# Seven block products of sums in place of eight for the lookups of an image, with the differences on GpSimd and one ring of eight PSUM banks

## The chip, the cores and the metric

The kernel runs on one core of one Trainium2 chip. The metric is the device time of one execution in microseconds; "before" is the median of three runs.

## The reference

A pre-activation block of two convolutions in which each 3x3 convolution is replaced by a soft lookup. For every channel the 3x3 patch is compared with 16 centroids of 9 values, a softmax over the 16 distances gives weights, and the weights select from a table of 256 outputs.

```python
def amm_conv3x3(x, centroids, w_sub):
    p = patches                                  # [b, n, c, 9]
    d = sum(p*p) - 2*einsum('bncs,cks->bnck', p, centroids) + sum(centroids**2)
    attn = softmax(-d, axis=-1)                  # 16 weights a channel
    lut = einsum('cks,cso->cko', centroids, w_sub)
    return einsum('bnck,cko->bno', attn, lut)

def layer(x):                                    # [16, 256, 28, 28] float32
    out = amm_conv3x3(groupnorm(x), centroids1, wsub1)
    out = relu(bn1(out))
    out = amm_conv3x3(out, centroids2, wsub2)
    out = se(bn2(out))
    return x + relu(out + groupnorm(x))
```

## The kernel before

The sum over centroids is moved in front of the table: a channel's 9 weighted centroid values (a "numerator" each) are divided by the softmax's denominator, and the 256 x 9 quotients of a position are multiplied by `w_sub` (2304 x 256). So an image of a layer is a matrix product of the quotients with `w_sub`, and that product is called the lookup.

**Blocks.** The work of one layer and one image is cut into four blocks: two halves `t` of the 28 rows (14 rows, N = 392 positions) and two halves `hh` of the 256 input channels. A block's quotients are nine tiles q of 128x392 (k = 0 to 8). There are 2 layers x 16 images x 4 = 128 blocks, layer by layer, image by image.

**Order.** All five engines execute one order written out by hand: `at(cluster, place, function, ...)` (L657) files a job under a cluster and a place in it, and the jobs are then issued sorted by both. Each engine takes its own instructions in that order and waits for what it needs. A block j begins in cluster g = 2j, and each cluster does half of a block's logits; an image takes eight clusters. Below, "even" and "odd" clusters are those of the first and the second half of a block. A block passes through:

- `patches` (L283): six DMAs on SP's queue load the shifted rows of 64 channels from a DRAM copy of the padded image (`home1` or `home2`) into one of three patch buffers, three clusters ahead.
- `logits` (L298, cluster g and g+1): 32x32 matmuls into four banks for each quarter `mm` of the block, eight banks a cluster; `exps` (L312) takes the exponential of each bank on ScalarE. In layer 1, for the first quarter of a block with hh = 0, the logits are first copied, turned, reduced to a maximum, reduced by it and turned back on VectorE (`wide_copy`, `wide_turn`, `wide_sub`, `wide_back`, `wide_exp`).
- `num_b`, `split_b`, `join_b`, `recip_dve` (even cluster g+2): the denominators r and the ninth numerator; the join and the reciprocal are on VectorE. Then `spread` (a shuffle of r to the lanes of tile k) and `scale_q` (q times the spread r, both in SBUF), for k = 8.
- `num_a` (L348): the other eight numerators, four banks in cluster g+2 that ScalarE copies (`copy_a`; they are scaled in cluster g+3 by four pairs of `spread` and `scale_q`), and four in cluster g+3 that VectorE multiplies straight from PSUM (`scale_a`).
- `lookup` (L428): for each half t of the rows and each half o of the 256 outputs, nine matmuls of 128x128 by 128x392 for each hh go into one accumulator bank. An image has eight such groups of nine, one a cluster in clusters 5 to 12 counted from the image's first, at place 2.0, after logits and numerators. `evacuate` (L438) reads an accumulator with scale, bias and, in layer 0, ReLU, on ScalarE, at the head of the next cluster.

PSUM has eight banks: one for the accumulator (`p_acc`) and a ring of seven (`p_ring`), which are taken in turn.

**Beside it.** GpSimd normalises the next image (`gn_apply`) and sends stores to DRAM from its own queue: the padded image, the layer-0 results (`to_home2`, an indirect DMA whose row order is a ranking of channels by size). The ranking is made once from image 0: `rank_score`, `rank_row`, `rank_make` and `rank_look` around cluster 13, and the tables of layer 1 are then re-ordered (`prep_codes`, `prep_sub`, `prep_wd0` to `prep_cwb`). In layer 1 `se_hidden`, `se_gate`, `finish` (L640) and `store` end an image: one ScalarE and two VectorE instructions of 128x784 for each half of the outputs.

After the 256 clusters a flag is computed; a loop that does the whole work more slowly (and safely) stands behind it and is not entered with these inputs.

Of the kernel before, what the change touches and what calls it, by code (L numbers as in the profile page):

```python
# [8 lines left out]
F32 = mybir.dt.float32  # L9
# [27 lines left out]
NPT = 3  # L37
# [21 lines left out]
def kernel(  # L59
# [27 lines left out]
    p_acc = ctx.enter_context(tc.tile_pool(name="p_acc", bufs=1, space=PSUM))  # L87
    p_ring = ctx.enter_context(tc.tile_pool(name="p_ring", bufs=7, space=PSUM))
# [23 lines left out]
    d_fl = dram.tile([1, 1], I32, name="d_fl")  # L112
# [5 lines left out]
    epool = ctx.enter_context(tc.tile_pool(name="epool", bufs=24))  # L118
    qpool = ctx.enter_context(tc.tile_pool(name="qpool", bufs=27))
# [4 lines left out]
    def load_x(b, eng=None):  # L124
        t = io.tile([P, NB, HW], F32, tag="xt", name="xt")
        (eng or nc.sync).dma_start(t, x[b].rearrange("(b p) n -> p b n", p=P))
        xs[b] = t
# [22 lines left out]
    def load_ws(l, hh, eng=None):  # L150
        t = wpool.tile([P, NS, C], F32, tag=f"ws{hh}", name=f"ws{hh}")
        eng = eng or nc.sync
        if l == 0:
            eng.dma_start(t, ws1[:, NS * hh : NS * hh + NS, :])
        else:
            eng.dma_start(t[:, 0:8, :], view(d_wa, hh * 8 * P * C, [[C, P], [P * C, 8], [1, C]]))
            eng.dma_start(t[:, 8, :], d_wb[hh * P : hh * P + P, :])
        wts["ws", hh] = t
# [4 lines left out]
    kst = load(konst, "kst")  # L163
    load_cw(0, 0)
# [17 lines left out]
    xpad = io.tile([P, NB, NPAD], F32, tag="pa", name="xpad")  # L182
    hpads = [io.tile([P, NPAD], F32, tag="pc", name="hpad", bufs=3) for _ in range(NB)]
# [4 lines left out]
    nc.vector.memset(xpad[:, 0], 0.0)  # L188
    nc.gpsimd.memset(xpad[:, 1], 0.0)
# [26 lines left out]
    def center(wf, n):  # L216
        for c0 in range(0, n, 384):
            w = min(384, n - c0)
            sq = rpool.tile([P, N], F32, tag="xy", name="sq")
# [7 lines left out]
        nc.vector.tensor_sub(g, g, cst[:, : n // K].unsqueeze(2).to_broadcast([P, n // K, K]))  # L227

# [39 lines left out]
    def gn_apply(b, k, eng=None):  # L268
        xt = xs[b]
        (eng or nc.gpsimd).tensor_scalar(  # L270
            grid(xpad[:, k])[:, 1 : H + 1, 1 : W + 1], xt[:, k].rearrange("p (r w) -> p r w", w=W),
# [6 lines left out]
    def to_home1(b, k, eng=None):  # L278
        if k == NB - 1:
            xs.pop(b)  # L280
        (eng or nc.gpsimd).dma_start(home1[b][k * P : (k + 1) * P], twice(xpad[:, k]))

    def patches(u, p, eng=None):  # L283
# [3 lines left out]
        eng = eng or nc.sync  # L287
        for dy in range(3):
            eng.dma_start(
# [3 lines left out]
            eng.dma_start(  # L293
# [18 lines left out]
    def exps(u, mm):  # L312
        es = []
        for bk in u.pop(("lg", mm)):
            e = epool.tile([P, N], F32, tag="e", name="e")
            nc.scalar.activation(e, bk[:, :N], AF.Exp, scale=2.0)  # L316
            es.append(e)
        u["e", mm] = es

    def wide_copy(u, mm):  # L320
        raw = io.tile([P, 4 * N], F32, tag="pa", name="raw")
        for i, bk in enumerate(u.pop(("lg", mm))):
            nc.scalar.copy(raw[:, N * i : N * i + N], bk[:, :N])  # L323
        u["raw", mm] = raw

    def wide_turn(u, mm):
        z = io.tile([P, 4 * N], F32, tag="pb", name="z")
        nc.vector.transpose(z, u["raw", mm])
# [5 lines left out]
    def wide_sub(u, mm):  # L334
        z, mx = u["z", mm]
        zk = z.rearrange("p (g k) -> p g k", k=K)
        nc.vector.tensor_sub(zk, zk, mx.unsqueeze(2).to_broadcast([P, N // 4, K]))

    def wide_back(u, mm):
        z, _ = u.pop(("z", mm))  # L340
        nc.vector.transpose(u["raw", mm], z)  # L341

    def wide_exp(u, mm):
        raw = u.pop(("raw", mm))
        nc.scalar.activation(raw, raw, AF.Exp, scale=2.0)  # L345
        u["e", mm] = [raw[:, N * i : N * i + N] for i in range(4)]

    def num_a(u, mm):  # L348
        bs = [bank("na") for _ in range(2)]
        es = u["e", mm]  # L350
        for i in range(4):
            for r in range(2):
# [3 lines left out]
                    rhs=es[i][64 * r : 64 * r + 64, :],  # L356
# [4 lines left out]
    def num_b(u):  # L361
        bs = [bank("nb") for _ in range(2)]
        for mm in range(4):
            es = u["e", mm]
            for i in range(4):
                for r in range(2):
# [3 lines left out]
                        rhs=es[i][64 * r : 64 * r + 64, :],  # L370
# [4 lines left out]
    def split_b(u):  # L375
        b0, _ = u["nb"]
        y = rpool.tile([P, N], F32, tag="xy", name="y")
        nc.scalar.activation(y, b0[:, :N], AF.Identity, bias=zero, scale=m_hi)  # L378
# [575 lines left out]
```

## Time and profile before

| | us |
|---|---|
| median of 3 runs | 3015.77 (3012.92 to 3015.99) |
| profiled execution, its own time | 2994.09 |
| its span, first to last instruction | 2992.6 |
| TensorE busy | 2927.7 (98%) |
| VectorE busy | 2067.1 (69%) |
| ScalarE busy | 1361.1 (45%) |
| GpSimd busy | 251.8 (8%) |
| DMA engines, mean share of the 16 | 51% in those 90.2 us of layer 0, 47% in those 93.0 us of layer 1 (next row) |
| VectorE busy in 90.2 us of layer 0 / 93.0 us of layer 1 | 55.9 / 72.8 |

In the rows of the profile PE is TensorE's matmuls, PEld its weight loads, DVE VectorE, ACT ScalarE, POOL GpSimd and SP SyncE. A group's row gives the line, the engine and operation, output and input tiles, shapes, the count, then the busy time in us and the mean of one in ns, and after the second bar the idle time before it and what ended most of it. `[0.31 <-ACT e L316]` in a timeline means that the engine stood for 0.31 us until that instruction's end. The granted TensorE clock was 0.992 of full speed in the mean. Instructions of one engine overlap at their ends, so a sum of durations is a little above the time that they hold the engine: shuffles recorded at 0.59 us start every 0.50 us.

### The profile page before, as it was taken

The numbers are of one execution on the slowest core, as the hardware profiler recorded it, in microseconds if no ns is written. First come the engines' busy times: TensorE is split into PE (matmuls) and PEld (weight loads), VectorE is DVE, ScalarE is ACT, GpSimd is POOL, SyncE is SP. The second block draws the span as 40 slices with busy tenths as digits, with TensorE's granted clock in tenths as the row PEclk, the third lists the DMA queues.
The fourth block names the chain that finished last, engine by engine and source line by source line (L and its number), as shares of the span: only waits on it lengthen the run. The fifth ranks groups of instructions, "written<-read, shape, count | busy, mean of one in ns | idle before, by whom it ended". The sixth has DMA issues, their size and how long they took to land.

```text
span 2992.6 us, 87885 instructions
## 1 busy us (share of the span) xinstructions
PE 2927.7 (98%) x37648; PEld 1424.0 (48%) x37648; DVE 2067.1 (69%) x4480; ACT 1361.1 (45%) x3122; POOL 251.8 (8%) x273
## 2 busy tenths in 40 slices
PE   5989999999999999999999999999999999999997
PEld 2434444444444444444444444444444444444444
DVE  5756567666665665665577787787787777877785
ACT  3434444444444444444444554445554454554542
POOL 2022311111101111011000000000000000000000
PEclk9989999999999999999999999999999999999999
DMA  8556655555555555555554444444453444544440
GB/s 213 131 134 161 176 130 148 146 145 138 118 139 136 143 139 138 118 139 129 127 149 99 112 103 103 100 104 108 107 113 90 103 109 105 110 105 100 93 100 34
DMA packets 197357, 366.18 MB, mean 122 GB/s; under 512 B 22312, under 2 KB 172376, under 8 KB 196704
## 3 DMA queue, kind: packets, MB, share of 16 engines
q1 hardware_dynamic: 184416, 295.35, 44.0%
q0 software_dynamic: 12544, 65.12, 6.2%
q8 instruction: 300, 4.92, 0.7%
q14 instruction: 97, 0.79, 0.1%
HBM read 283.86 MB, written 76.51 MB: 120 GB/s over the span
## 4 chain that ended last, share of the span: by engine, by line
PE 96%; DMA 2%; DVE 1%; issue 0%; POOL 0%; ACT 0%; SPq 0%; POOLq 0%; ACTq 0%; DVEq 0%
PE acc L431 52%; PE lg L303 19%; PE na L353 12%; PE nb L367 12%; DMA pt<-home 1%; DMA d_sc<-score 0%; PE sep L628 0%; DMA row<-d_sc 0%; DMA home<-hpad,hidx 0%; POOL xpad L270 0%; PE gnp L246 0%; PE gnp L257 0%; DMA home<-xpad 0%; PE sep L615 0%; DVE gn_st L240 0%
## 5 line engine op out<-in xcount | busy, mean ns | idle before, releaser
L431 PE MATMUL acc<-q,ws 128*128 128x392 f32 x4608 | 1584.5, 498 | 0.9 <-ACT y L452 0.9
L431 PEld LDWEIGHTS acc<-q,ws 128*128 128x128 f32 x4608 | 855.3, 190 | 724.4 <-issue 151.1
L316 ACT ACTIVATE e<-lg 128x392 f32<-128x392 f32 x1920 | 777.5, 530 | 498.7 <-PE lg L303 487.7
L407 DVE STREAM_SHUFFLE rb<-r 128x392 f32<-128x392 f32 x1152 | 645.1, 593 | 0.0
L303 PE MATMUL lg<-pt,wd 32*32 32x392 f32 x16384 | 613.0, 502 | 21.6 <-ACT e L316 9.7
L423 DVE TENSOR_TENSOR q<-na,rb 128x392 f32<-128x392 f32 x512 | 252.8, 555 | 245.8 <-PE na L353 245.8
L303 PEld LDWEIGHTS lg<-pt,wd 32*32 32x32 f32 x16384 | 244.7, 103 | 333.7 <-issue 187.6
L411 DVE TENSOR_TENSOR q<-q,rb 128x392 f32<-128x392 f32 x640 | 363.2, 567 | 53.7 <-DVE rb L407 0.9
L388 DVE SCALAR_TENSOR_TENSOR r<-nb,kst,y 128x392 f32<-128x392 f32 x128 | 80.0, 625 | 458.6 <-ACT y L378 442.8
L353 PE MATMUL na<-e,cwa 64*32 64x392 f32 x7680 | 387.2, 497 | 0.0
L367 PE MATMUL nb<-e,cwb 64*32 64x392 f32 x7680 | 349.9, 497 | 0.0
L397 DVE RECIPROCAL r<-r 128x392 f32<-128x392 f32 x128 | 331.9, 2593 | 0.0
L353 PEld LDWEIGHTS na<-e,cwa 64*32 64x32 f32 x7680 | 141.6, 106 | 209.7 <-ACT e L316 106.7
L367 PEld LDWEIGHTS nb<-e,cwb 64*32 64x32 f32 x7680 | 142.2, 108 | 185.3 <-issue 124.2
L416 ACT COPY q<-na 128x392 f32<-128x392 f32 x512 | 210.1, 506 | 0.0
L442 ACT ACTIVATE hpad<-acc,bnsh,bnsc 128x392 f32<-128x392 f32 x64 | 43.5, 680 | 313.6 <-PE acc L431 293.4
L378 ACT ACTIVATE y<-nb,kst 128x392 f32<-128x392 f32 x128 | 86.7, 677 | 167.2 <-PE nb L367 167.2
L452 ACT ACTIVATE y<-acc,bnsh,bnsc 128x392 f32<-128x392 f32 x64 | 43.4, 678 | 240.4 <-PE acc L431 240.4
L323 ACT COPY raw<-lg 128x392 f32<-128x392 f32 x128 | 52.9, 500 | 191.2 <-PE lg L303 184.4
L461 POOL DMA_INDIRECT home<-hpad,hidx x64 | 63.8, 998 | 889.7 <-ACT hpad L442 737.8
L345 ACT ACTIVATE raw<-raw 128x1568 f32<-128x1568 f32 x32 | 48.4, 1511 | 112.4 <-DVE raw L341 112.4
L270 POOL TENSOR_SCALAR xpad<-xt,nrm 128x784 f32<-128x784 f32 x30 | 90.9, 3030 | 0.0
(134 smaller groups left out, 878.6 us busy)
## 6 DMA issues: line engine op xcount, KB each, us to landing
pt<-home SPq DMA_DIRECT2D x768, 209.0 KB
pt<-home SPq DMA_DIRECT2D x768, 104.5 KB
home<-xpad POOLq DMA_DIRECT2D x30, 899.0 KB, 5.2
xt<-in_x SPq DMA_DIRECT2D x32, 784.0 KB
out_dram<-y SPq DMA_DIRECT2D x32, 392.0 KB
ws<-in_ws SPq DMA_DIRECT2D x2, 1152.0 KB
st<-in_wsub POOLq DMA_DIRECT2D x4, 512.0 KB, 6.9
ws<-d_wa SPq DMA_DIRECT2D x2, 1024.0 KB
```

The source lines that it names most:

```text
L270: (eng or nc.gpsimd).tensor_scalar(grid(xpad[:, k])[:, 1 : H + 1, 1 : W + 1], xt[:, k].rearrange("p (r w) -> p r w", w=W), nrm[:, b, 0, k ...
L303: nc.tensor.matmul(bk[32 * c : 32 * c + 32, :N].rearrange("p (r w) -> p r w", w=W), lhsT=wts["wd", u["hh"]][32 * i : 32 * i + 32, mm, c, : ...
L316: nc.scalar.activation(e, bk[:, :N], AF.Exp, scale=2.0)
L353: nc.tensor.matmul(bs[r][32 * i : 32 * i + 32, :N], lhsT=wts["cwa", u["hh"]][64 * r : 64 * r + 64, mm, i, :], rhs=es[i][64 * r : 64 * r + ...
L367: nc.tensor.matmul(bs[r][32 * i : 32 * i + 32, :N], lhsT=wts["cwb", u["hh"]][64 * r : 64 * r + 64, mm, i, :], rhs=es[i][64 * r : 64 * r + ...
L378: nc.scalar.activation(y, b0[:, :N], AF.Identity, bias=zero, scale=m_hi)
L397: nc.vector.reciprocal(u["r"], u["r"])
L407: nc.vector.stream_shuffle(rb, u["r"], mask_of(k))
L411: nc.vector.tensor_mul(u["q", k], u["q", k], u.pop(("rb", k)))
L416: nc.scalar.copy(q, bk[:, :N])
L423: nc.vector.tensor_mul(q, bk[:, :N], u.pop(("rb", k)))
L431: nc.tensor.matmul(accs[o][:, :N], lhsT=wts["ws", u["hh"]][:, k, o * P : (o + 1) * P], rhs=u["q", k], start=first, stop=last,)
```

## The change

**Products.** The four blocks of an image and the four quarters of `w_sub` form a 2x2 by 2x2 product of blocks. Strassen's scheme (in Winograd's form) does it in seven products of differences and sums. The 9 x 8 = 72 matmuls of an image become 9 x 7 = 63. The blocks are called in another order, (hh, t) = (0,0), (0,1), (1,1), (1,0).

**Differences.** Four times an image, nine tiles q of a block are replaced by a difference (`mix`, a subtraction of two 128x392 tiles in SBUF, on GpSimd): 36 an image. The sums of the weights (`combine`) are made once a layer on VectorE.

**Sums of the results.** The products are read out into the result tiles: two copies on ScalarE (`acc_copy`), seven additions or subtractions of a product to a result (`acc_add`, VectorE) and two sums of results (`reg_add`, one on GpSimd, one on VectorE); then `norm_out` does scale, bias and ReLU on ScalarE from SBUF.

**PSUM.** The accumulator comes out of the same ring, which now has eight banks.

**Other moves.** Two patch buffers for three, filled two clusters ahead; `wide_turn` and `wide_sub` earlier, and one of two subtractions on GpSimd; the second VectorE instruction of `finish` becomes a ReLU on ScalarE and an addition on GpSimd a cluster later, and the store follows one more cluster later; loads and stores of the ranking and the re-ordered tables from GpSimd's queue to SP's, with image 0's layer-0 result kept in DRAM (`d_h0`) and put in place once the ranking is there; image 1 is loaded at the start, and half of the first patches are issued by GpSimd. The q tiles are 33 fixed buffers with an assignment worked out ahead (`homes`).

```diff
-NPT = 3
+NPT = 2
+KO = (8, 4, 5, 6, 7, 0, 1, 2, 3)
+BLOCKS = ((0, 0), (0, 1), (1, 1), (1, 0))
+PRODUCTS = {
+    5: ("A11", 0, KO), 6: ("S1", 0, KO[:4]), 7: ("S1", 0, KO[4:]), 8: ("S3", 1, KO), 9: ("S4", 2, KO),
+    10: ("S2", 0, KO), 11: ("A12", 3, KO), 12: ("A22", 0, KO),
+}
...
-    p_acc = ctx.enter_context(tc.tile_pool(name="p_acc", bufs=1, space=PSUM))
-    p_ring = ctx.enter_context(tc.tile_pool(name="p_ring", bufs=7, space=PSUM))
+    p_ring = ctx.enter_context(tc.tile_pool(name="p_ring", bufs=8, space=PSUM))
...
+    def combine(n):
+        a, b, op = {
+            "S1": ("S3", "A22", ALU.add), "S2": ("S1", "A11", ALU.subtract),
+            "S4": ("A12", "S2", ALU.subtract), "S3": ("A11", "S3", ALU.subtract),
+        }[n]
+        nc.vector.tensor_tensor(wl[n], wl[a], wl[b], op)
...
+    def product(key, us, w, ks, first=True, last=True):
         if first:
-            accs[o] = p_acc.tile([P, 512], F32, tag="acc", name="acc")
-        nc.tensor.matmul(
-            accs[o][:, :N], lhsT=wts["ws", u["hh"]][:, k, o * P : (o + 1) * P], rhs=u["q", k],
-            start=first, stop=last,
-        )
+            accs[key] = bank("acc")
+        for n, k in enumerate(ks):
+            nc.tensor.matmul(
+                accs[key][:, :N], lhsT=wl[w][:, k, :], rhs=us["q", k],
+                start=first and n == 0, stop=last and n == len(ks) - 1,
+            )
+
+    def mix(out_u, k, in0, in1):
+        nc.gpsimd.tensor_tensor(out_u["q", k], in0["q", k], in1["q", k], ALU.subtract)
...
+    def acc_add(l, b, o, t, key, o2=None, t2=None, op=ALU.add, pop=True):
+        other = region(l, b, o if o2 is None else o2, t if t2 is None else t2)
+        if op == ALU.add:
+            nc.vector.tensor_tensor(region(l, b, o, t), acc_of(l, key), other, op)
...
-                    at(g, 1.9, wide_turn, u, mm)
-                    at(g + 1, 0.8, wide_sub, u, mm)
-                    at(g + 1, 0.81, wide_back, u, mm)
-                    at(g + 1, 1.95, wide_exp, u, mm)
+                    at(g, 0.9, wide_turn, u, mm)
+                    at(g, 0.95, wide_sub, u, mm, nc.gpsimd if u["r"] == 1 else None)
+                    at(g + 1, 0.3, wide_back, u, mm)
+                    at(g + 1, 0.9, wide_exp, u, mm)
...
+            for c, (w, r, ks) in PRODUCTS.items():
+                at(g + c, 2.0, product, (n, c), us[r], w, ks)
+            for k in KO:
+                at(g + 5, 2.5, mix, us[0], k, us[1], us[0])
+            for k in KO:
+                at(g + 7, 2.5, mix, us[1], k, us[2], us[1])
+            for k in KO:
+                at(g + 7, 2.6, mix, us[0], k, us[2], us[0])
+            for k in KO:
+                at(g + 10, 2.5, mix, us[0], k, us[0], us[3])
+            at(g + 6, 0.0, acc_copy, l, b, 0, 0, (n, 5))
+            at(g + 7, 0.0, acc_copy, l, b, 1, 1, (n, 6))
+            at(g + 8, 0.0, acc_add, l, b, 1, 1, (n, 7))
+            at(g + 8, 0.01, reg_add, l, b, (0, 1), (0, 0), (1, 1), nc.gpsimd)
+            at(g + 9, 0.0, acc_add, l, b, 1, 0, (n, 8), 0, 0)
+            at(g + 10, 0.0, acc_add, l, b, 0, 1, (n, 9))
+            at(g + 11, 0.0, acc_add, l, b, 1, 0, (n, 10), pop=False)
+            at(g + 11, 0.01, acc_add, l, b, 0, 1, (n, 10))
+            at(g + 11, 0.02, reg_add, l, b, (1, 1), (1, 1), (1, 0), nc.vector)
...
+            at(g + 12, 0.0, acc_add, l, b, 0, 0, (n, 11))
+            at(g + 13, 0.0, acc_add, l, b, 1, 0, (n, 12), op=ALU.subtract)
...
+                    at(g + 15, 0.9 + 0.01 * q, finish_gate, b, q)
+                    at(g + 15, 1.9 + 0.01 * q, finish_norm, b, q)
+                    if b < B - 1:
+                        at(g + 16, 0.9, finish_relu, b, q)
+                        at(g + 16, 1.0, finish_add, b, q)
+                        at(g + 17, 0.6, store, b, q)
```

## Prediction

> **What bounds the kernel now.** I read the page first, then the chain of waits in a stretch of layer 0, then the timeline there.
>
> ```profile
> PE 2927.7 (98%) x37648; PEld 1424.0 (48%) x37648; DVE 2067.1 (69%) x4480; ACT 1361.1 (45%) x3122; POOL 251.8 (8%) x273
> ...
> L431 PE MATMUL acc<-q,ws 128*128 128x392 f32 x4608 | 1584.5, 498 | 0.9 <-ACT y L452 0.9
> ...
> L411 DVE TENSOR_TENSOR q<-q,rb 128x392 f32<-128x392 f32 x640 | 363.2, 567 | 53.7 <-DVE rb L407 0.9
> ...
> L270 POOL TENSOR_SCALAR xpad<-xt,nrm 128x784 f32<-128x784 f32 x30 | 90.9, 3030 | 0.0
> ```
>
> TensorE is the bound and GpSimd is nearly idle. The lookups (L431) are 256 x 9 written matmuls, but x4608: each is two instructions of 1584.5/4608 = 0.344 us. The chain shows the rhythm of two clusters:
>
> ```profile
> 1418.72 2.33 PE lg L303 x63
> 1421.05 2.79 PE nb L367 x64
> 1423.84 1.32 PE na L353 x32
> 1425.16 6.12 PE acc L431 x18
> 1431.28 2.27 PE lg L303 x62
> 1433.55 1.58 PE na L353 x32
> 1435.13 6.12 PE acc L431 x18
> ```
>
> An even cluster takes 12.56 us, an odd one 9.97, an image 4 x 22.53 = 90.1. The timeline shows what the 98% hides:
>
> ```profile
> 1418.65 2.40 PE L303 MATMUL lg<-pt,wd 32*32 32x392 f32 x64
> ...
> 1420.18 0.15 PEld L303 LDWEIGHTS lg<-pt,wd 32*32 32x32 f32 x8 [0.31 <-ACT e L316]
> 1420.97 0.18 PEld L367 LDWEIGHTS nb<-e,cwb 64*32 64x32 f32 x16 [0.64 <-ACT e L316]
> ...
> 1424.64 0.62 DVE L388 SCALAR_TENSOR_TENSOR r<-nb,kst,y 128x392 f32<-128x392 f32 x1 [6.00 <-ACT y L378]
> ...
> 1430.99 0.59 DVE L407 STREAM_SHUFFLE rb<-r 128x392 f32<-128x392 f32 x1
> ...
> 1434.46 1.98 DVE L423 TENSOR_TENSOR q<-na,rb 128x392 f32<-128x392 f32 x4 [2.87 <-PE na L353]
> ...
> 1440.62 0.57 DVE L411 TENSOR_TENSOR q<-q,rb 128x392 f32<-128x392 f32 x1
> ```
>
> The eighth logit bank (the last x8) waits for the first one's exponential, since the ring has seven banks, and nb then waits for the third (two nb banks, one ring turn on). VectorE ends its even work at 12.83 us after the cluster's start (1431.48), its odd work at 9.9: at the end of the product both times. It works for as long as TensorE does, with a pause before each join.
>
> **What the Trainium skill says.** "Perfetto Trace Analysis", Identifying the Most-Contended Engine: matmul busy share says little of how close TensorE is to its peak; the 0.31 and 0.64 us above agree. "GPSIMD Engine Reference", Elementwise: a two-input f32 add of 2048 elements takes 4497 ns there. No such row is in this trace (L270 is one input, 3.03 us for 784, where that page calls one input about line-rate, so the trace differs). "SBUF — State Buffer", Who interferes with whom: a VectorE instruction with two SBUF inputs and a GpSimd instruction that reads SBUF exclude each other for the whole instruction. L411 is such an instruction. In 15 places it starts while L270 is still recorded, and its durations stay 566 to 571 ns; but all 15 lie in the last 0.4 us of L270, so this neither shows nor refutes it.
>
> **The change, part by part.**
>
> 1. Lookups: 288 matmuls fewer, 576 x 0.344 = 198 us, 6.19 per image (I use 6.12, the chain's). All of it is on TensorE's path. But clusters 6 and 7 of an image now share one product (4 and 5 matmuls).
>
> 2. One ring of eight. Logits' last bank now follows the product's bank, and nb or na follow logits 1 and 2, not 2 and 3. Exponentials are 0.40 us apart, so nb/na can start 1.9 us after the cluster's start, not 2.3: -0.4 us for each of 8 clusters, if the product's bank is read out within 1.7 us of its end. Where it is read at T, nb starts at T+0.2.
>
> 3. Read-out. ScalarE copies two products (0.5 us, it waits there anyway: 6.8 us before L316). VectorE adds the rest: 7 of about 0.55 us (nearest row: the PSUM product L423, 555 ns; 0.5 to 0.7), plus one region add on VectorE, one on GpSimd. Each stands behind the whole VectorE work of its cluster, and logits' eighth bank stands behind it.
>
> 4. Clusters 6 and 7. From cluster 6's start: nb 1.9 to 4.75, join at 5.54, VectorE even work 6.84 to 12.38, four scale_a to 14.29, four pairs of shuffle and scale_q at 1.185 to 19.03, read-out 19.65. TensorE is done with cluster 7 at 8.72+6.9 = 15.6, so T = 4.05 and nb waits to 4.25 where it was 2.3 before: +1.95. In layer 1, finish_norm (two, 1.9 us) and the gate (0.35) lie between: T = 6.3, +4.2.
>
> 5. Other clusters, GpSimd costing VectorE nothing: layer 0 all -0.4 (two read-outs and the batch statistics just fit). Layer 1: turn, reduce and subtract (5.47 us) now stand before the join, so cluster 1 +0.4, cluster 3 +0.1, the others -0.4. Image sums: layer 0 -6.12+1.95-7x0.4 = -7.0; layer 1 -6.12+4.2+0.4+0.1-5x0.4 = -3.4. Times 16 each: **-166**.
>
> 6. GpSimd: 36 differences per image. From the skill, 4497 x 392/2048 = 0.86 plus a fixed 0.19 (row nrm 128x2): 1.05 us, an estimate, 38 us of an 80 us image. From L270: 1.5 us, 55 us. Either fits: each mix has one to two clusters before its product. I take 1.05. What it costs VectorE is unknown: nothing, to the full exclusion. In clusters 5, 7 and partly 1 and 3, four scale_q fall among mixes back to back; with exclusion a pair lasts 1.05+0.5 = 1.55, not 1.185, and the first waits up to 1 us: about +2.0 per four. Then in layer 0 cluster 0 has +3.95 and the seven others -0.2 on average: -3.6. In layer 1 cluster 0 has +7.0 (finish_norm waits too), clusters 1, 3, 4 have +1.4, +0.8, +0.9, the rest -1.2: +2.8. Times 16: **-13**. A gain below "nothing" is excluded, since GpSimd takes no VectorE work but one wide subtraction per image (1.8 us, counted).
>
> 7. The ranking. Before, TensorE stood for 13.5 us in the window 150 to 200 (busy 36.5 of 50):
>
> ```profile
> 164.44 9.98 DMA d_sc<-score
> ...
> 175.00 7.04 DMA row<-d_sc
> ```
>
> These waits now lie on SP; VectorE's rank_make (5 us) stays, in cluster 15: **-8**.
>
> 8. At no cost: two patch buffers for three (six issues of 0.6 us and 5.6 us of transfer, half of a cluster at 50% DMA share, so 8 us; the shortest window, clusters 6 and 7, leaves 14; without it TensorE would wait the difference). About 40 issues moved from GpSimd to SP, 0.55 us each over 45 clusters, while SP idles 1474 us for logits; the row's 10 us wait lies behind cluster 14's patches and before cluster 15's. On GpSimd, the home stores now queue behind up to 19 us of mixes; they are read images later. ReLU and add of the finish lie on ScalarE (45%) and GpSimd a cluster later, and the store on SP behind them, after that cluster's patches. combine (4 x 1.3 us, from 1.79 for 1568 elements) lies before the first products, and once in VectorE's pause of cluster 6. Start: the early load of image 1 and split issue, -5 to +5.
>
> Sum: between -174 and -21. **I take half of the exclusion: -98**, since a mix must often wait for a scale_q itself and so is not always there. The profiled run's own time was 2994.09 (span 2992.6 and 1.5 around it), so it would be 2896. The median of the runs is 21.7 us above that run, so I forecast 2918.
>
> **Rivals.**
>
> A. VectorE and GpSimd don't disturb each other: -174, so 2842. For it: 15 overlaps without lengthening. Against: all at the very end of L270.
>
> B. Full exclusion at 1.05 us: -21, 2995. For it: the skill's sentence. VectorE would then be the bound in layer 1: 73.5 us of work per image by the durations above, and some 10 of waiting, against 80 on TensorE.
>
> C. Slower. A mix takes 1.5 us, as L270 has it, and excludes scale_q: a pair lasts 2.05 us, four cost +3.5 and not +2.0. The read-out that opens cluster 0 then comes 1.5 us later in both layers, the other clusters lose 1 (layer 0) to 2.5 (layer 1) together: (2.5+4) x 16 = +104 on B, 3099. It decides from a mean wait of about 0.6 us per scale_q (+2.4 per four): there the gain is gone. For it: the only GpSimd row of size. Against: one input with two scalars and rows of 28 is not a mix.
>
> **Numbers.** Chances: forecast 0.45, A 0.2, B 0.13, C 0.22. Of B a part is within 0.2% (6 us, about what a measurement can tell from no change) or above. So faster 0.74, same 0.04, slower 0.22. The range runs from below A, less 15 for the start and the read-out's lower bound, to between B and C: 2825 to 3045.
>
> **What would show it.** L431's successor with 4032 instructions; na and nb starting 1.9 us after logits in clusters 1 to 7 (step 2); TensorE waiting for VectorE's read-out at the eighth bank of cluster 0 of each image, 2 to 4 us in layer 0 and 4 to 7 in layer 1 (step 4); mixes 1.05 us apart (step 6); scale_q lengthened or late beside them; no gap at 165 to 185 (step 7). It would be wrong if TensorE waits for q (a mix), for pt, or if layer 1 loses more than layer 0 gains.

## The result and the profile after

The changed kernel takes 3117.2 us (median, 3114.01 to 3119.5) against 3014.77 before: 1.034 times as long, 95% interval 1.0322 to 1.0358. It is slower, by 102 us where a gain of 98 was forecast. Its profiled execution has a span of 3115.6 us, and the granted TensorE clock is 0.953 in the mean where it was 0.992.

The engines' busy time, the chain and two groups of the page of after:

```profile
PE 2845.3 (91%) x37072; PEld 1313.2 (42%) x37072; DVE 2383.1 (76%) x4698; ACT 1405.2 (45%) x3216; POOL 1643.0 (53%) x1482
...
PE 62%; DVE 28%; issue 3%; ACT 3%; DMA 2%; POOL 2%; SPq 0%; another core or an unknown queue 0%; DVEq 0%; POOLq 0%; ACTq 0%
...
L450 POOL TENSOR_TENSOR qs<-qs,qs 128x392 f32<-128x392 f32 x1152 | 1270.6, 1140 | 783.2 <-PE acc L444 621.6
...
L424 DVE TENSOR_TENSOR qs<-qs,rb 128x392 f32<-128x392 f32 x640 | 537.3, 840 | 54.4 <-DVE rb L420 0.9
```

TensorE has 576 instructions fewer, as it should. But it now stands for 270 us of the span (3115.6 - 2845.3; before 65), and the chain that ended last runs through VectorE for 28% of it. The differences (L450) take 1140 ns in the mean, and `scale_q` (L424) went from 567 to 840 ns in the mean. For whom TensorE waits stands in the waits of after (us in total, times, longest):

```profile
PEld lg L323 <- DVE y L472: 116.5, 55, 6.1
PEld lg L323 <- DVE hpad L472: 112.6, 52, 10.0
...
PE lg L323 <- DVE hpad L472: 85.1, 38, 9.3
PEld acc L444 <- POOL qs L450: 85.0, 86, 5.9
PE lg L323 <- DVE y L472: 83.6, 29, 5.4
```

L472 is the read-out by VectorE (`acc_add`), into hpad in layer 0 and y in layer 1: logits' eighth bank waits for it. The fourth line is a product that waits for a difference. (PE and PEld lines of one wait overlap and are not added.)

The table has the length of an image and of its clusters, from one start of logits on TensorE to the next, as medians over images 5 to 13 of layer 0 and 3 to 14 of layer 1. Clusters 6 and 7 are those that share a product. "Ratio" is to the kernel before on the same chip. The runs e1 to e15 are told in the next section.

| kernel | ratio (95%) | layer 0: image | cl. 0 | cl. 1 | cl. 6 | layer 1: image | cl. 0 | cl. 1 |
|---|---|---|---|---|---|---|---|---|
| before | 1 | 90.7 | 12.6 | 10.0 | 12.6 | 90.9 | 12.5 | 10.0 |
| after | 1.034 (1.0322 to 1.0358) | 98.1 | 20.2 | 10.3 | 13.3 | 92.5 | 20.5 | 10.0 |
| e1_no_mix | 0.9811 (0.9791 to 0.983) | 90.0 | 13.8 | 9.6 | 8.9 | 88.5 | 17.9 | 9.6 |
| e2_write_only | 1.004 (1.0027 to 1.0052) | 92.8 | 14.3 | 9.6 | 14.6 | 89.3 | 18.1 | 10.3 |
| e3_gap | 1.0332 (1.0315 to 1.0349) | 96.0 | 19.0 | 9.9 | 13.4 | 92.2 | 21.0 | 9.6 |
| e4_ring7 | 1.0037 (1.0023 to 1.0051) | 89.5 | 12.6 | 10.0 | 13.2 | 92.1 | 13.2 | 16.4 |
| e5_early | 1.0292 (1.0264 to 1.032) | 92.7 | 14.4 | 10.1 | 14.0 | 93.9 | 12.3 | 19.5 |
| e9_hpad2 | 1.0802 (1.0769 to 1.0835) | 105.6 | 19.2 | 23.2 | 8.9 | 92.5 | 20.4 | 10.2 |
| e10_hpad2_early | 1.075 (1.0704 to 1.0795) | 105.4 | 20.4 | 22.5 | 8.9 | 93.9 | 12.3 | 19.5 |
| e11_hpad2_early_pool8 | 1.0931 (1.0913 to 1.0949) | 104.6 | 30.4 | 10.6 | 8.9 | 95.6 | 12.2 | 22.5 |
| e12_store_order | 1.0196 (1.0153 to 1.024) | 93.3 | 18.5 | 10.0 | 8.9 | 92.5 | 20.5 | 10.0 |
| e13_ring7_store | 0.986 (0.9843 to 0.9876) | 86.1 | 12.6 | 10.0 | 9.3 | 92.1 | 13.1 | 16.5 |
| e14_layer0_only | 0.9807 (0.979 to 0.9823) | 86.0 | 12.6 | 10.0 | 9.3 | 90.9 | 12.5 | 10.0 |
| e15_no_norm | 0.9636 (0.962 to 0.9652) | 88.2 | 12.6 | 10.0 | 9.3 | 85.9 | 12.5 | 10.9 |

So after loses 7.4 us an image in layer 0 and 1.6 in layer 1. The loss stands in cluster 0 (+7.6 and +8.0), and in layer 0 cluster 6, which has five of nine matmuls fewer, is no shorter. The timeline of after at the change from cluster 7 to cluster 0, layer 1:

```profile
2413.57 1.93 PE L323 MATMUL lg<-pt,wd 32*32 32x392 f32 x56
...
2416.89 3.49 DVE L701 SCALAR_TENSOR_TENSOR y<-xt,nrm,y 128x784 f32<-128x784 f32 x2
...
2420.30 0.55 DVE L472 TENSOR_TENSOR y<-acc,y 128x392 f32<-128x392 f32 x1
...
2420.91 1.53 PE L323 MATMUL lg<-pt,wd 32*32 32x392 f32 x8 [5.40 <-DVE y L472]
...
2422.37 4.19 PE L384 MATMUL nb<-e,cwb 64*32 64x392 f32 x64
```

The first 56 logits go at once, the last x8 waits 5.40 us for the read-out, which stands behind finish_norm (L701). Then x8 and nb are slow themselves: nb takes 4.19 us, and 2.86 us otherwise. The same place in an image of layer 0, with what happens from cluster 6 on:

```profile
990.56 0.98 POOL L499 DMA_INDIRECT home<-hpad,col  x1 [6.25 <-DVE r L404]
...
991.56 8.81 POOL L450 TENSOR_TENSOR qs<-qs,qs 128x392 f32<-128x392 f32 x9
...
992.63 3.83 PE L444 MATMUL acc<-qs,w_S 128*128 128x392 f32 x8 [2.35 <-POOL qs L450]
...
994.14 6.66 DVE L424 TENSOR_TENSOR qs<-qs,rb 128x392 f32<-128x392 f32 x1
...
997.21 0.49 ACT L466 COPY hpad<-acc 128x392 f32<-128x392 f32 x1 [5.37 <-PE acc L444]
...
1009.70 0.56 DVE L472 TENSOR_TENSOR hpad<-acc,hpad 128x392 f32<-128x392 f32 x1
...
1010.31 1.53 PE L323 MATMUL lg<-pt,wd 32*32 32x392 f32 x8 [4.71 <-DVE hpad L472]
```

Three things are in it. The nine differences that are filed under cluster 5 begin only here in cluster 6, after the home store (L499), so product 6 (L444) waits for them. One `scale_q` (L424) is recorded for 6.66 us, until the burst of nine differences is over (1000.37); below, such a `scale_q` is called held. And so VectorE's read-out for cluster 0 is late as well.

### The profile page after: what moved, and what is told of

It reads as the page before. It is cut to its first block, busy times and chain, and to the rows that moved or that the text cites. A ratio compares the mean times of both kernels' runs of the same rounds, so it can differ in the third digit from the quotient of the medians.

```text
span 3115.6 us, 89074 instructions
## 1 busy us (share of the span) xinstructions
PE 2845.3 (91%) x37072; PEld 1313.2 (42%) x37072; DVE 2383.1 (76%) x4698; ACT 1405.2 (45%) x3216; POOL 1643.0 (53%) x1482
## 4 chain that ended last, share of the span: by engine, by line
PE 62%; DVE 28%; issue 3%; ACT 3%; DMA 2%; POOL 2%; SPq 0%; another core or an unknown queue 0%; DVEq 0%; POOLq 0%; ACTq 0%
PE acc L444 29%; PE lg L323 13%; PE nb L384 12%; DVE rb L420 7%; PE na L370 7%; DVE qs L424 6%; DVE r L410 5%; DVE y L701 2%; DVE qs L436 2%; ACT r L395 1%; DVE r L404 1%; DVE qs L407 1%; DVE hpad L472 1%; DMA home<-hpad,col 1%; POOL xpad L291 1%
## 5 line engine op out<-in xcount | busy, mean ns | idle before, releaser
L450 POOL TENSOR_TENSOR qs<-qs,qs 128x392 f32<-128x392 f32 x1152 | 1270.6, 1140 | 783.2 <-PE acc L444 621.6
L444 PE MATMUL acc<-qs,w_S 128*128 128x392 f32 x2304 | 822.1, 508 | 34.0 <-POOL qs L450 33.2
L444 PEld LDWEIGHTS acc<-qs,w_S 128*128 128x128 f32 x2304 | 430.7, 193 | 428.3 <-POOL qs L450 85.0
L444 PE MATMUL acc<-qs,w_A 128*128 128x392 f32 x1728 | 595.5, 499 | 0.0
L424 DVE TENSOR_TENSOR qs<-qs,rb 128x392 f32<-128x392 f32 x640 | 537.3, 840 | 54.4 <-DVE rb L420 0.9
L444 PEld LDWEIGHTS acc<-qs,w_A 128*128 128x128 f32 x1728 | 321.5, 190 | 274.6 <-ACT e L335 39.6
L404 DVE SCALAR_TENSOR_TENSOR r<-nb,kst,r 128x392 f32<-128x392 f32 x128 | 79.9, 624 | 414.0 <-ACT r L395 404.0
L436 DVE TENSOR_TENSOR qs<-na,rb 128x392 f32<-128x392 f32 x512 | 252.7, 554 | 99.8 <-PE na L370 98.1
L499 POOL DMA_INDIRECT home<-hpad,col x60 | 60.4, 1006 | 370.2 <-ACT hpad L486 185.4
L430 ACT COPY qs<-na 128x392 f32<-128x392 f32 x512 | 210.5, 505 | 12.9 <-PE na L370 12.7
L395 ACT ACTIVATE r<-nb,kst 128x392 f32<-128x392 f32 x128 | 86.7, 678 | 208.1 <-PE nb L384 186.0
```

What stands on the lines that cost most here:

```text
L395: nc.scalar.activation(r, b0[:, :N], AF.Identity, bias=zero, scale=m_hi)
L424: nc.vector.tensor_mul(u["q", k], u["q", k], u.pop(("rb", k)))
L430: nc.scalar.copy(u["q", k], bk[:, :N])
L436: nc.vector.tensor_mul(u["q", k], bk[:, :N], u.pop(("rb", k)))
L444: nc.tensor.matmul(accs[key][:, :N], lhsT=wl[w][:, k, :], rhs=us["q", k], start=first and n == 0, stop=last and n == len(ks) - 1,)
L450: nc.gpsimd.tensor_tensor(out_u["q", k], in0["q", k], in1["q", k], ALU.subtract)
```

## The experiments

Ahead of each measurement stands what was expected of the run; it names theories and rivals by letters.

**Differences left out (e1_no_mix).** The products then use tiles that are not differences; a scale is lowered so that the values stay small.

```diff
-        nc.gpsimd.tensor_tensor(out_u["q", k], in0["q", k], in1["q", k], ALU.subtract)
+        return
```

> The changed kernel without the 1152 differences on GpSimd (left out: the products read the undifferenced q, and batch norm 1 is scaled by 0.05 so that the values stay small). Theory S (the VectorE instructions with two SBUF inputs stand behind GpSimd's reads, so the read-outs come late): with nothing on GpSimd to stand behind, scale_q is back at 568 ns everywhere, cluster 6 of layer 0 falls from 13.4 to about 8.8 us, cluster 0 from 20 to 14.5 (layer 0) and 17 (layer 1), and the time is 2830 to 2900. Rival L (the two short clusters and the place of the read-out in the ring are enough by themselves): it stays above 3020.

Measured: 2939.33 us, ratio 0.9811, between the ranges of S and L. `scale_q` is back at 572 ns, and the lengths of clusters 0 and 6 are about those of theory S. The differences cost 5.3% of the time in all. But the gain without them, 57 us, is a third of the 166 that was worked out for a GpSimd that costs nothing: the seven products' order alone keeps cluster 0 of layer 1 at 17.9 us, and in layer 0 the store still stands in ScalarE's way, which writes the same result tile again. The waits of e1:

```profile
PE lg L325 <- DVE y L474: 47.6, 15, 3.3
ACT hpad L468 <- DMA home<-hpad,col: 42.3, 8, 5.8
```

**GpSimd that only writes (e2_write_only).** Each difference is replaced by three memsets of its tile, about 1.3 us together.

```diff
-        nc.gpsimd.tensor_tensor(out_u["q", k], in0["q", k], in1["q", k], ALU.subtract)
+        for _ in range(3):
+            nc.gpsimd.memset(out_u["q", k], 0.5)
```

> Each difference is replaced by three GpSimd memsets of the same tile (so GpSimd is busy for about as long, in the same places of its queue and with the same waits for the products, but reads no SBUF; the values are constants, batch norm 1 scaled by 0.05). Theory S: it is the reading that counts, so scale_q stays at 568 ns and the time is within 1.5% of the kernel without differences, 2830 to 2930. Rival Q (GpSimd's queue: TensorE or the next job waits for GpSimd being busy): about as the changed kernel, 3050 to 3120.

Measured: ratio 1.004 (3006.45 us), again between the two ranges. `scale_q` has a mean of 606 ns and a longest of 1.87 us, where after has 14 of over 3 us. So the long ones come from GpSimd's reading, not from its work or its writes. But cluster 6 of layer 0 is 14.6 us: with no contention to speak of, product 6 waits for GpSimd all the same. The memsets are slower than the differences, so the run gives no size for this wait; but it pointed to what stands ahead in GpSimd's queue.

**A pause after each difference (e3_gap).**

```diff
+    gap = const.tile([P, 1], F32, name="gap")
...
         nc.gpsimd.tensor_tensor(out_u["q", k], in0["q", k], in1["q", k], ALU.subtract)
+        nc.gpsimd.memset(gap, 0.0)
```

> After each difference GpSimd sets one column of a small tile (about 0.1 us, writes only), so that no two differences follow each other directly. Theory S in its burst form (a waiting VectorE instruction gets in only when GpSimd leaves a hole): scale_q never lasts over 2 us, cluster 6 of layer 0 falls from 13.4 to below 10 us, and the time is 3000 to 3060. If the small write is no hole, or the long waits have another cause, scale_q still reaches 6 us and the time is 3110 to 3140.

Measured: ratio 1.0332, as after, with 14 `scale_q` of over 3 us left, up to 9.9 us. The timeline of e3, in a place where VectorE does get in:

```profile
990.80 1.30 POOL L452 TENSOR_TENSOR qs<-qs,qs 128x392 f32<-128x392 f32 x1
...
991.85 0.68 DVE L424 TENSOR_TENSOR qs<-qs,rb 128x392 f32<-128x392 f32 x1
...
992.04 0.09 POOL L453 MEMSET gap<- 128x1 f32 x1
992.10 1.30 POOL L452 TENSOR_TENSOR qs<-qs,qs 128x392 f32<-128x392 f32 x1
```

The memset (L453) begins before the difference ahead of it is recorded as done, and the next difference 0.06 us later. It opened no hole, so this run can't say whether a hole would always let VectorE in.

**The products' own bank again (e4_ring7).**

```diff
-    p_ring = ctx.enter_context(tc.tile_pool(name="p_ring", bufs=8, space=PSUM))
+    p_acc = ctx.enter_context(tc.tile_pool(name="p_acc", bufs=1, space=PSUM))
+    p_ring = ctx.enter_context(tc.tile_pool(name="p_ring", bufs=7, space=PSUM))
...
-            accs[key] = bank("acc")
+            accs[key] = p_acc.tile([P, 512], F32, tag="acc", name="acc")
```

> One part undone: the products get their own bank again and the ring has seven banks. If step 2 of the prediction is right (the eighth bank is worth 0.4 us a cluster where the read-out is in time) and the late read-out is what cluster 0 waits for: na and nb start 2.3 us after the logits again (+0.4 x 7 clusters x 32 = +90), but cluster 0's logits no longer wait for VectorE's read-out, only its product does, 4 us later (-4 to -8 x 32): 2950 to 3080. If cluster 0 waits for something else (a difference, q, the patches), it keeps its 20 us and the time is 3180 to 3220.

Measured: ratio 1.0037, so the shared ring makes 3 of the 3.4%. In layer 0 cluster 0 is 12.6 us, as before the change: what needs the read-out now is the next product, which comes some 5 us after logits' eighth bank. In layer 1 the wait only moves: cluster 0 falls by 7.3 us and cluster 1 grows by 6.4.

**The read-out earlier (e5_early).** The read-out that opens cluster 0 is put between the pairs of cluster 7, with two of them and finish_norm behind it.

```diff
-            at(g + 8, 0.0, acc_add, l, b, 1, 1, (n, 7))
+            at(g + 7, 2.05, acc_add, l, b, 1, 1, (n, 7))
...
-                    at(g + 15, 1.9 + 0.01 * q, finish_norm, b, q)
+                    at(g + 15, (2.2 if b < B - 1 else 1.9) + 0.01 * q, finish_norm, b, q)
```

> The read-out of the fifth-cluster-pair's product 7 moves forward on VectorE, from behind all work of cluster 7 to between its second and third pair of spread and scale_q (finish_norm goes behind it too). Theory R (cluster 0's TensorE wait is VectorE reaching this read-out late, and its half clock follows from that wait): cluster 0 falls from 20 to 13 to 15 us in both layers, the granted clock rises above 0.97, and the ratio to the kernel before goes from 1.034 to 0.97 to 0.99. Rival (cluster 0 waits for something else behind it, so the wait moves to cluster 1): the sum of clusters 0 and 1 stays at 30 and the ratio above 1.02.

Measured: ratio 1.0292. Layer 0 gains 5.4 us an image. In layer 1 cluster 0 is 12.3 us and cluster 1 is 19.5, in sum 31.8 against 30.5 in after, as the rival had it: VectorE's work that was passed over is missing one read-out later.

**All stores behind the differences (e9_hpad2, e10, e11).** hpad exists twice, for even and odd images, and the four home stores of an image move behind the differences of cluster 5.

```diff
-    hpads = [io.tile([P, NPAD], F32, tag="pc", name="hpad", bufs=4) for _ in range(NB)]
+    hpads = [io.tile([P, NPAD], F32, tag="pc", name="hpad", bufs=6) for _ in range(2 * NB)]
...
-                        at(g + 12 + o, 0.5, to_home2, b, o)
+                        at(g + 13, 2.55 + 0.01 * o, to_home2, b, o)
```

> The two layer-0 result tiles become two sets, by image in turn, and the stores to_home2 of an image go behind the nine differences of cluster 5 in GpSimd's queue (room for the tiles: 32 q tiles for 33 and four rb for five). Theory H (in layer 0 the differences of cluster 5 stand behind two indirect stores, the second of which waits 5 us for the first to land, so product 6 waits for GpSimd and ScalarE's copy for the stores): cluster 6 of layer 0 falls from 13.3 to about 9 us and the long scale_q of cluster 6 goes; layer 1 stays as it is (92.5 an image); ratio to before 0.98 to 1.01. Rival (cluster 6 is long because its scale_q stands behind the differences wherever those lie): cluster 6 stays above 12 us, ratio 1.025 to 1.035.

Measured: ratio 1.0802. Theory H holds for cluster 6 alone: it is 8.9 us, so the stores were what made it late. But the layer-0 image is 105.6 us, since the same stores now stand before the differences of cluster 7, as the timeline of e9 shows:

```profile
1021.88 1.08 POOL L499 DMA_INDIRECT home<-hpad,col  x1 [0.16 <-issue]
1028.85 0.99 POOL L499 DMA_INDIRECT home<-hpad,col  x1 [5.89 <-DMA home<-hpad,col]
1035.31 0.97 POOL L499 DMA_INDIRECT home<-hpad,col  x1 [5.48 <-ACT e L335]
1040.74 0.97 POOL L499 DMA_INDIRECT home<-hpad,col  x1 [4.46 <-DMA home<-hpad,col]
1041.73 17.50 POOL L450 TENSOR_TENSOR qs<-qs,qs 128x392 f32<-128x392 f32 x18
...
1045.27 15.36 DVE L424 TENSOR_TENSOR qs<-qs,rb 128x392 f32<-128x392 f32 x1
```

Four stores to one DRAM tensor hold the queue for 20 us: each waits for the one before to land (so the profile puts it for two of the three), about 6 us. Then eighteen differences stand in one run, and a `scale_q` is held for 15.36 us, until the run and GpSimd's region add behind it are over. Cluster 1 is 23.2 us. With the earlier read-out of e5 as well:

> Both of the last two edits. Theories H and R together: the two waits lie in different clusters, so their gains add: layer 0 about 86, layer 1 about 86 us an image, ratio to before 0.94 to 0.97. Rival (one late engine behind both: what is taken from one cluster comes back in another): no better than the better of the two alone.

Measured: 1.075, the two effects side by side. And with the ninth tile's `scale_q` on GpSimd in addition:

> As the last, and the scale_q of tile 8 (one a block, four an image) goes from VectorE to GpSimd. Theory S (this scale_q is the one that stands behind differences and delays VectorE's even clusters): another 0.5 to 1% off. Rival (after the two edits VectorE is in time anyway, or GpSimd's queue is now the later one): within 0.5% of the last, or slower.

Measured: 1.0931, worse. That multiplication then waits in GpSimd's queue, and the tile is the first that a product wants: cluster 0 of layer 0 is 30.4 us, cluster 1 of layer 1 22.5.

**One store behind the differences (e12_store_order).** As e9, but only the fourth store moves, so that none waits for a landing while differences are due.

```diff
-    def to_home2(b, o, src=None):
-        for r in range(2):
+    def to_home2(b, o, src=None, rs=(0, 1)):
+        for r in rs:
...
-                        at(g + 12 + o, 0.5, to_home2, b, o)
+                        at(g + 12 + o, 0.5, to_home2, b, o, rs=(0, 1)[: 2 - o])
+                        if o:
+                            at(g + 13, 2.55, to_home2, b, o, rs=(1,))
```

> Edit: the result tiles hpad exist twice (even and odd images), and of the four home stores of a layer-0 image only the last one (second half of the channels, second row shift) is moved behind the nine differences of cluster 5; the other three stay where the changed kernel has them. Theory S (the serial home stores ahead of cluster 5's differences on GpSimd make product 6 late, and through it ScalarE's first copy and the burst of differences that holds scale_q): the differences start one landing, 6 us, earlier, cluster 6 of a layer-0 image falls from 13.3 to 9-10 us, no wait of TensorE for a difference in cluster 6 is left, scale_q over 3 us become fewer than 5 and the layer-0 image goes from 98.1 to 92-94 us. Layer 1 stays at 92.5. Ratio 1.00 to 1.02 against the kernel before. Rival T (the store that is moved only makes the next differences late, as it did when all four were moved): cluster 1 of layer 0 goes above 15 us, the layer-0 image stays at 97 or more, ratio 1.03 or more.

Measured: 3069.78 us, ratio 1.0196. Cluster 6 is 8.9 us and the image 93.3: theory S. One part of it missed: 15 `scale_q` of over 3 us are left, now in cluster 5 (10 of them) and elsewhere. The burst still holds one, only a cluster earlier, where no product waits for it. But VectorE's read-out for cluster 0 is late all the same. The timeline of e12 has the eighth bank of cluster 0 after a held `scale_q` (the first line, of 8.95 us) and in one of the two images in which none was held before it:

```profile
858.96 8.95 DVE L424 TENSOR_TENSOR qs<-qs,rb 128x392 f32<-128x392 f32 x1
...
882.25 0.98 PE L323 MATMUL lg<-pt,wd 32*32 32x392 f32 x8 [3.94 <-DVE hpad L472]
...
973.03 0.86 PE L323 MATMUL lg<-pt,wd 32*32 32x392 f32 x8 [1.69 <-DVE hpad L472]
```

Cluster 0 takes 14.6 us in both of these two images (10 and 11), and 18.5 to 20.2 in images 7, 8, 9, 12, 13 and 14, each of which follows a held one. With the shared ring, then, a held `scale_q` in cluster 5 still costs cluster 0 some 4 to 6 us.

**Store order and own bank (e13_ring7_store).** e12 and e4 together.

> Edit: the store order and doubled hpad of the run before, and the products get their own PSUM bank again beside a ring of seven, as in the kernel before. Theory R (two separate costs in layer 0: logits' last bank waits for the read-out, 7.6 us a layer-0 image, and the stores in front of the differences, about 5 us): the gains add up, no cluster 0 of layer 0 above 14 us, the layer-0 image 85 to 88 us; layer 1 at 92 us as with the ring of seven alone. Ratio 0.98 to 0.99. Rival V (VectorE beside GpSimd's reading is the limit in layer 0 as well, so that a stall taken away only moves): the layer-0 image stays at 89.5 or more as with the ring of seven alone, ratio 1.00 to 1.01.

Measured: 2973.93 us, ratio 0.986, with 86.1 and 92.1 us an image: theory R. In layer 0 the two costs are separate and add up. Layer 1 is where e4 left it. The timeline of e13, TensorE in clusters 0 and 1 of layer 1, and then the windows of the same place, whose columns are length, busy time of PE, PEld, DVE, ACT and POOL, the granted clock, the DMA share and GB/s:

```profile
2277.76 2.63 PE L324 MATMUL lg<-pt,wd 32*32 32x392 f32 x64
2280.32 1.55 PE L371 MATMUL na<-e,cwa 64*32 64x392 f32 x32
2285.24 9.11 PE L445 MATMUL acc<-qs,w_S 128*128 128x392 f32 x18 [3.37 <-DVE y L473]
```

```profile
2282.00:2285.24 3.24, 0.01 (x1) 0.01 (x1) 3.24 (x11) 0.00 (x0) 3.24 (x3) 0.86 0.91 176
2285.24:2288.00 2.76, 2.76 (x4) 1.50 (x5) 2.76 (x4) 1.01 (x1) 1.96 (x2) 0.50 0.78 205
2288.00:2291.00 3.00, 3.00 (x6) 1.69 (x5) 2.79 (x8) 0.51 (x1) 0.00 (x0) 0.50 1.02 334
2291.00:2294.30 3.30, 3.30 (x14) 1.54 (x12) 2.31 (x7) 0.00 (x0) 0.00 (x0) 0.98 0.32 125
```

The product waits 3.37 us for the read-out, in which VectorE is busy throughout, and then takes 9.11 us where 6.19 is usual, since the clock is at 0.50 for some 6 us.

**Seven products in layer 0 alone (e14_layer0_only).** e13, and layer 1 with the eight products of the kernel before.

```diff
+            if l == 0:
                 for c, (w, r, ks) in PRODUCTS.items():
...
+            else:
+                k = g + 5
+                for t in range(2):
+                    for o in range(2):
+                        for hh in range(2):
+                            name = (("A11", "A12"), ("S3", "A22"))[o][hh]
+                            at(k, 2.0, product, (n, t, o), us[2 * t + hh], name, KO, hh == 0, hh == 1)
+                            k += 1
+                        at(k, 0.0, norm_acc, l, b, o, t, (n, t, o))
...
-    for n, m in enumerate(("S1", "S2", "S4", "S3")):
-        at(g + 6, 0.05, combine, m)
```

> Edit: the run before (store order, products' own bank, ring of seven), and the seven-product form only in layer 0; layer 1 does the eight products of the kernel before, two clusters to one accumulator, read out by ScalarE from PSUM, without differences and without sums of weights, with both wide subtractions of an image on GpSimd. Theory L (layer 1 has no room on VectorE for the seven-product form; with eight products TensorE is the limit there as before): the layer-1 image goes from 92 to 90-91 us, layer 0 stays at 85 to 88, ratio 0.97 to 0.98, faster than the kernel before. Rival M (layer 1 is slow from something else of the change, such as the earlier wide reduction or the finish on GpSimd): the layer-1 image stays at 92 or more, ratio no lower than with seven products in both layers.

Measured: 2957.26 us, ratio 0.9807, faster than both kernels by more than their intervals. Layer 1 is at 90.9 us, cluster for cluster as before the change: theory L. The timeline of e14 in layer 0:

```profile
732.19 8.64 DVE L427 TENSOR_TENSOR qs<-qs,rb 128x392 f32<-128x392 f32 x1
732.54 7.87 POOL L453 TENSOR_TENSOR qs<-qs,qs 128x392 f32<-128x392 f32 x8
732.70 2.40 PE L326 MATMUL lg<-pt,wd 32*32 32x392 f32 x64
735.03 2.87 PE L387 MATMUL nb<-e,cwb 64*32 64x392 f32 x64
737.69 1.52 PE L373 MATMUL na<-e,cwa 64*32 64x392 f32 x32
739.14 2.90 PE L447 MATMUL acc<-qs,w_S 128*128 128x392 f32 x8
```

`scale_q` is held for 8.64 us here too, and TensorE goes on without a stop: there is no bank that it waits for and no tile that it lacks. 16 x 4.7 us are 75; 59 are measured. Images 1 to 6 take 52 us more than six at the median (before: 24). Of these, 39 lie in clusters 9, 16, 43, 44, 48 and 49, where VectorE's single work for the ranking and the re-ordered tables stands ahead of a read-out or of statistics that TensorE waits for (in front of cluster 16 `rank_make`, 11.7 us, and then a product waits 9.49 us), and 7 in cluster 24, after a held `scale_q`. No run moved this work.

**VectorE's work in layer 1 (e15_no_norm).** e13, with one addition of the finish left out.

```diff
-                    at(g + 15, 1.9 + 0.01 * q, finish_norm, b, q)
+                    if b == B - 1:
+                        at(g + 15, 1.9 + 0.01 * q, finish_norm, b, q)
```

> Edit: the run with the products' own bank and the store order (seven products in both layers), with one VectorE instruction of the finish left out, twice an image in layer 1 but the last: the addition of the normalised image (128x784, 1.73 us each, so 3.5 us of VectorE an image). Theory V (in layer 1 VectorE works without a pause from cluster 6 to cluster 1, and TensorE's long cluster 1 is what that is late): cluster 1 of a layer-1 image falls one for one, from 16.5 to 13 us, the image from 92.1 to 88.5-89.5, the ratio from 0.986 to about 0.969-0.973. Rival O (the order of the read-outs in the clusters makes TensorE wait, however much work stands before them): cluster 1 stays above 15 us, the image at 91 or more, ratio 0.98 or more.

Measured: ratio 0.9636, a layer-1 image of 85.9 us. 3.5 us less on VectorE take 6.2 us off the image, more than one for one and more than was expected: cluster 1 is 10.9 us. What is left of its wait in the timeline of e15:

```profile
2248.69 1.65 PE L371 MATMUL na<-e,cwa 64*32 64x392 f32 x32
2251.20 6.19 PE L445 MATMUL acc<-qs,w_S 128*128 128x392 f32 x18 [0.86 <-DVE y L473]
```

0.86 us for 3.37, and the product at full clock again (6.19 for 9.11): 2.5 and 2.9 us, and these are cluster 1's 5.6 nearly. Theory V, with the clock as the part that it lacked.

## Why the prediction was wrong

**Steps 1, 2 and 7** held. The instructions are fewer; where the read-out is in time, clusters take 9.6 and 12.2 us, 0.4 less than 9.97 and 12.56; in the window 150 to 200 TensorE is busy for 46.5 us, where it was 36.5. The start gave more than its -5 to +5: cluster 8 begins at 93.7 us and not at 102.0.

**Step 8 failed, and with it layer 0's cluster 6.** It put the home stores at no cost because their images are read late. What the stores write is in time; what stands behind them is late. Each store waits for the landing of the store before, and cluster 5's differences, and in e9 cluster 7's, stand behind that wait on GpSimd. So clusters 6 and 7 of layer 0 became 2.3 us shorter together, and not 6.9. e12 shows the step: one store moved, cluster 6 from 13.3 to 8.9 us, the image 4.8 us shorter. (The result tiles were doubled in the same run; doubling alone was not run, but in after product 6 waits for a difference, as shown above, and in e12 no longer.) The prediction's own list of what would make it wrong had the sign, "if TensorE waits for q (a mix)"; its working looked at who reads what the stores write, and not at who is queued behind them.

**Step 4: the mechanism was right, and so was the size without contention; the clock after the wait was put at nothing.** TensorE waits at the eighth bank of cluster 0, behind finish_norm in layer 1, as written, but cluster 0 is 7.6 us longer in layer 0 (forecast 1.95 without contention, 3.95 with exclusion) and 8.0 in layer 1 (4.2 and 7.0). In e12's two images without a held `scale_q` the read-out ends 3.6 us after the cluster's start, against T = 4.05, and cluster 0 takes 14.6 us, against 12.56 + 1.95. In after, in the layer-0 place above, it ends at 6.6 (1003.62 to 1010.26), after a held one. In layer 1 it ends 7.3 us after the cluster's start (2413.57 to 2420.85) against T = 6.3: beside the differences finish_norm's two instructions take 3.49 us, where the working had 1.9, and in e1, without the differences, they take 1.97:

```profile
2086.19 1.97 DVE L703 SCALAR_TENSOR_TENSOR y<-xt,nrm,y 128x784 f32<-128x784 f32 x2
...
2088.70 0.86 PE L325 MATMUL lg<-pt,wd 32*32 32x392 f32 x8 [3.28 <-DVE y L474]
...
2090.10:2093.50 3.40, 3.40 (x49) 1.34 (x41) 3.33 (x3) 1.51 (x3) 2.55 (x2) 0.50 0.66 146
```

The rest is the clock, which no step had. The Trainium skill, "TensorE: Matmul & The Clock Gate", HAM oscillation — how this bites in real kernels, names waits above about 3.4 us as those after which TensorE runs at half its clock. The runs show half the clock after waits, but not that limit. In e1 the fourteen waits of 3.25 to 3.28 us in cluster 0 of layer 1 are each followed by a stretch at 0.50 (the last two lines above are one of them), in after some waits of 2 to 3 us are, and in e13 two of about 3.4 are not. The windows of after around a wait of 9.32 us in layer 0:

```profile
306.00:311.87 5.87, 0.00 (x0) 0.00 (x0) 5.50 (x11) 0.00 (x0) 3.60 (x5) 0.50 0.91 202
311.87:313.33 1.46, 1.46 (x8) 0.20 (x9) 0.00 (x0) 0.00 (x0) 1.46 (x2) 0.50 1.04 201
313.33:316.00 2.67, 2.67 (x44) 0.94 (x48) 0.00 (x0) 0.50 (x1) 2.67 (x4) 0.50 0.72 218
316.00:318.80 2.80, 2.80 (x48) 1.04 (x40) 0.00 (x0) 0.00 (x0) 2.80 (x4) 0.50 0.94 162
318.80:322.00 3.20, 3.20 (x39) 1.31 (x22) 2.39 (x4) 2.78 (x6) 3.06 (x4) 0.95 0.38 96
```

For 6.9 us after the wait the clock is 0.50, which costs half of it, 3.5 us; in the place of layer 1 shown above it is 0.50 for 1.5 us and 0.68 in the mean for 4.2, which costs 2.1. So the slow clock added 2 to 3.5 us to the wait in these places.

**Step 6: the price was right, the model of the contention was not.** The estimate of 1.05 us for a difference, from the Trainium skill's "GPSIMD Engine Reference", Elementwise, was measured as 1.03 (median), and 0.98 from start to start in a burst. The skill's "SBUF — State Buffer", Who interferes with whom, has a full exclusion of the two engines for one whole instruction. The trace shows two regimes, and neither is the prediction's half or that exclusion. In step with each other, as in e3's lines, a difference takes 1.30 us and the `scale_q` beside it 0.68, and in after too a pair of shuffle and `scale_q` then comes every 1.30 us: 0.46 more per four pairs (4 x (1.30 - 1.185)), not 2.0. Out of step, once in nearly every layer-0 image, one `scale_q` is held, not until the difference under way ends but until the whole burst is over: 4.6 to 9.4 us in after, and up to 18.7 in e9, with its bursts of eighteen. What decides between them stays open; e3 was to open a hole and didn't. In after that burst fell on cluster 6, since the stores had put it there (step 8), and its delay added to cluster 0. In e12 and e14 it falls on cluster 5 and is as long; in e12 it still makes cluster 0 late, in e14, with the products' own bank, it costs TensorE nothing. And the forecast priced `scale_q` and finish_norm alone: beside the differences VectorE's region add, 0.56 us in e1, takes 1.3, and the wide subtraction, 1.79 us before, takes 2.4.

**Step 5: layer 1 has a second limit.** The forecast had +0.4 and +0.1 for its clusters 1 and 3, and only rival B had VectorE as the bound, by its total of 73.5 us in 80. But the work isn't spread evenly: from cluster 6 to cluster 1 VectorE has the finish, the wide reduction and the read-outs, and there it works almost without a pause (in e13 from 2261 to 2293: 31.3 of 32 us). The differences lengthen that work, finish_norm above all. e5 and e4 move the wait from cluster 0 to cluster 1 and leave the sum; e15 takes work out and the wait goes; e14 takes the seven products out and the layer is as before.

**The sum.** Layer 0 was to be 7.0 us an image shorter before contention, and its clusters are 6.8 longer in sum (the medians of the eight): 5.7 of the difference lie in cluster 0, 4.7 in clusters 6 and 7, 3.5 in the five others. Layer 1 was to be 3.4 shorter and is 1.6 longer: 3.8 in cluster 0, 1.2 in the others. Rival C, 3099 us, comes near the 3117 by luck, with the right sign and the wrong cause: a difference alone takes 1.03 us and not 1.5, and `scale_q` lost 0.27 us in the mean, not 0.6.

## What to carry to other kernels

When work is given to an idle engine, look at what already waits in that engine's queue, not only at its busy share: a store of 1 us can hold the queue for 6. A bank that is shared in a ring makes its slowest reader everyone's; a bank of its own for what is read out late was worth 3% here. Price a TensorE wait of about 3 us or more, and with some risk one of 2, with the slow clock after it. And where VectorE is to work beside GpSimd's two-input instructions, price every VectorE instruction that reads two SBUF tiles, not only the one that comes to mind.

## What the runs showed of the hardware that was not expected

- A VectorE multiplication of two SBUF tiles, 0.57 us alone, was held for up to 9.4 us beside a run of nine GpSimd subtractions of 1.03 us each and up to 18.7 beside a run of eighteen (e9), though each of these ended in between; beside GpSimd memsets it took 0.61 in the mean. A memset of one column between the subtractions changed nothing, but it opened no hole. An instruction of 128x784 with two SBUF inputs (finish_norm) was not held but went from 1.03 to 1.73 us in the mean.
- After most TensorE waits of 3.4 to 9.3 us the granted clock was 0.50 for some 3.4 to 7 us, and after waits of 3.25 to 3.28 us in e1 too; a product of nine took 9.11 us for 6.19.
- An indirect store from GpSimd took 5.7 us to land (median of e9), and in this program the next store of the image was issued only then: 5.4 to 7.0 us apart in the place shown, 20 us for four, with GpSimd standing.
